# Softmax sums of a chunk inverted on 128 partitions after a DMA, values and sums copied off PSUM by ScalarE

## The chip, the cores and the metric

The kernel runs on one core of a Trainium2 chip. The metric is the device time of one execution in microseconds (us). Before the change it is 6243.12 us, the median of 3 runs (6239.61 to 6246.1). The engines are named as the profile names them: PE (TensorE matmuls) and PEld (its weight loads), DVE (VectorE), ACT (ScalarE), POOL (GpSimd) and SP, whose queue issues the DMAs.

## The reference

Two layers over `x` of 8 batches x 2048 rows x 256 features, each wrapped in a residual and a layer norm, with one 2048 x 2048 adjacency matrix `adj`. What matters here is the first layer, attention with 4 heads of 64 features whose softmax is taken apart in each **chunk** of 256 keys and then summed over the 8 chunks:

```python
kc = k.reshape(B, H, Nc, CHUNK, Dh)
vc = v.reshape(B, H, Nc, CHUNK, Dh)
scores = jnp.einsum('bhnd,bhjcd->bhnjc', q, kc) / sqrt(Dh)
scores = jnp.clip(scores, -10.0, 10.0)
scores = jnp.where(mask == 0, -10.0, scores)
attn = jax.nn.softmax(scores, axis=-1)          # over c, in one chunk j
ctx = jnp.einsum('bhnjc,bhjcd->bhnd', attn, vc) # sum over j and c
out = ctx @ Wo.T + bo + x                       # then layer norm, residual, layer norm
```

So each query row, head and chunk has a sum of exponentials of its own, and the values of a chunk have to be divided by it before chunks are added. The second layer is a graph attention with one softmax over all 2048 keys; the change doesn't touch its lines.

## The kernel before

It is written in a framework in which the program states the work in order and a scheduler in the build places each engine's instructions: an instruction can be put ahead of an earlier one that isn't ready, while each engine executes its list strictly in order. Buffers come from pools: tiles of one tag share `bufs` buffers, and a new tile waits until an old one is released.

**Setup** (about 170 us): weights are transposed, and two int8 masks for all of `adj` are kept in SBUF. Then a loop over the 8 batches runs, each about 757 us:

- four `x` tiles of 512 rows are loaded (L215, pool `xp`, 5 buffers), transposed on PE (L204, tiles `p_xT`), and projected to keys (`pk`, L225) and values (`pv`, L234).
- **attention**, in four blocks `ib` of 512 queries. A block projects its queries (`pq`, L250) and then goes through 16 key tiles `c` of 128, two to a chunk. `scores(c)` makes, for each pair of heads, a tile `sc` of 128 keys x 2 heads x 512 queries in PSUM (L262), which DVE clips and masks in place (L270) and ACT exponentiates into `e` (L272). `values(c)` multiplies `e` with the values into `u` and with ones into `d` (L288): 12 calls with 32 output columns each, so that `u` (128 x 1024) and `d` (128 x 512) hold the four heads on 32 partitions each, and the 32 rows of a head in `d` are all equal to its sum. Both accumulate over the two key tiles of a chunk. The loop states scores(c) ahead of values(c-1).
- When a chunk `j` is complete, DVE takes the reciprocal of all of `d` (L297) and multiplies `u` with it straight from PSUM (L300 for the first chunk, L303 after), and POOL adds the product `un` to `ctxT` (L304).
- After 16 key tiles the block projects `ctxT` (`po`, L319); the residual and both layer norms follow on DVE and POOL (L326 to L332) and overwrite the block's `x` tile.
- **graph attention** in four blocks (L356 to L420), which reads the `x` tile of a block for the last time at L418. It loads rows of a mask (`fb`, L361) into buffers of the tag `ctx`, the one of `ctxT`.

[...] the tag `two` has 3 buffers of two banks each, shared by the `sc` and `u` tiles; the tag `m` has 2 buffers of one bank, shared by `d`, `po`, `pq`, `p_xT`, `pk`, `pv` and other small results. In the trace, tiles of the tag `m` get their buffers in the order in which the program states them: `pq` of the next block runs after `po` of this one (1810.84 after 1805.63 us), although it needs nothing of it.

The SP queue carries loads of `x`, loads of `fb` and stores of the output, none inside a block of attention but the first `fb`.

Of the kernel before, what the change touches and what calls it, by code (L numbers as in the profile page):

```python
# [9 lines left out]
F32 = mybir.dt.float32  # L10
# [7 lines left out]
DRAM = bass.MemoryType.DRAM  # L18

P = 128  # L20
# [8 lines left out]
def tile_adj_attention__then__gat(  # L29
# [27 lines left out]
    nc = tc.nc  # L57
    B, N, F = x.shape
    H, D = 4, 64
# [3 lines left out]
    IB = 512  # L63
# [4 lines left out]
    DH = D // 2  # L68
    QSCALE = 1.0 / D**0.5

    const = ctx.enter_context(tc.tile_pool(name="const", bufs=1))
    dram = ctx.enter_context(tc.tile_pool(name="dram", bufs=1, space=DRAM))

    ps_2 = ctx.enter_context(tc.tile_pool(name="ps_2", bufs=3, space=PSUM))
    ps_m = ctx.enter_context(tc.tile_pool(name="ps_m", bufs=2, space=PSUM))
# [38 lines left out]
    with tc.tile_pool(name="setup", bufs=2) as setup:  # L114
        for name, w in (("q", Wq), ("k", Wk), ("v", Wv), ("o", Wo)):
            wn = setup.tile([P, KC, F], F32, tag="wn", name=f"wn_{name}")
            if name == "o":
                by_half = w.rearrange("(o p) (h k m) -> p o k h m", p=P, h=H, k=2)
                for o in range(KC):
                    for k in range(2):  # L120
                        nc.sync.dma_start(
                            out=wn[:, o, ts(k, P)].rearrange("p (h m) -> p h m", h=H), in_=by_half[:, o, k]
# [11 lines left out]
        for n in range(2):  # L134
            a_bc = setup.tile([P, F], F32, tag="a_bc", name=f"a_bc{n}")
            nc.sync.dma_start(
                out=a_bc, in_=a[n * F : (n + 1) * F, :].rearrange("f o -> (f o)").partition_broadcast(P)
# [31 lines left out]
                    nc.vector.tensor_scalar(to, pt, hi - lo, lo, ALU.mult, ALU.add)  # L169

    big = ctx.enter_context(tc.tile_pool(name="big", bufs=1))
    xp = ctx.enter_context(tc.tile_pool(name="xp", bufs=5))
    wp = ctx.enter_context(tc.tile_pool(name="wp", bufs=2))
    rp = ctx.enter_context(tc.tile_pool(name="rp", bufs=1))
    ep = ctx.enter_context(tc.tile_pool(name="ep", bufs=4))
    sp = ctx.enter_context(tc.tile_pool(name="sp", bufs=3))

# [12 lines left out]
    def normalize(dst, src, name):  # L190
        mv, rstd = stats(src, name)
        for t in range(TPB):
            nc.vector.tensor_scalar(  # L193
                dst[:, t, :], src[:, t, :], mv[:, t, 0:1], rstd[:, t : t + 1], ALU.subtract, ALU.mult
            )
# [12 lines left out]
    def bc_rows(v):  # L208
        return v.unsqueeze(1).to_broadcast([P, TPB, F])

    for b in range(B):
# [33 lines left out]
        for ib in range(NIB):  # L245
            qT = wp.tile([P, NPAIR, IB], F32, tag="q", name=f"qT{b}_{ib}")
            for o in range(NPAIR):
                pq = ps_m.tile([P, IB], F32, tag="m", name=f"pq{b}_{ib}_{o}")
                for k in range(KC):
                    nc.tensor.matmul(  # L250
                        pq, WT["q"][:, k, ts(o, P)], xT[:, k, ts(ib, IB)], start=(k == 0), stop=(k == KC - 1)
                    )
                nc.scalar.activation(qT[:, o, :], pq, AF.Identity, bias=bq_c[:, o : o + 1], scale=QSCALE)  # L253

            ctxT = wp.tile([P, 2, IB], F32, tag="ctx", name=f"ctxT{b}_{ib}")

            def scores(c):
                es = []
                for hp in range(NPAIR):
                    sc = ps_2.tile([P, 2, IB], F32, tag="two", name=f"sc{b}_{ib}_{hp}_{c}")  # L260
                    for h in range(2):
                        nc.tensor.matmul(  # L262
                            sc[:, h, :],
                            kT[h * D : (h + 1) * D, hp, ts(c, P)],
                            qT[h * D : (h + 1) * D, hp, :],
                            start=True,
                            stop=True,
                        )
                    cap = mask0[:, c, ts(ib, IB)].unsqueeze(1).to_broadcast([P, 2, IB])
                    nc.vector.scalar_tensor_tensor(sc, sc, -CLIP, cap, ALU.max, ALU.min)  # L270
                    e = ep.tile([P, 2, IB], F32, tag="e", name=f"e{b}_{ib}_{hp}_{c}")
                    nc.scalar.activation(e, sc, AF.Exp)  # L272
                    es.append(e)
                return es

            ud = {}

            def values(c, es):
                j, first, last = c // CPT, c % CPT == 0, c % CPT == CPT - 1
                if first:  # L280
                    ud["u"] = ps_2.tile([P, 2, IB], F32, tag="two", name=f"u{b}_{ib}_{j}")
                    ud["d"] = ps_m.tile([P, IB], F32, tag="m", name=f"d{b}_{ib}_{j}")
                u, d = ud["u"], ud["d"]
                for part in range(3):
                    for h in range(H):
                        rows = slice(h * DH, (h + 1) * DH)
                        f0 = h * D + part * DH
                        nc.tensor.matmul(  # L288
                            u[rows, part, :] if part < 2 else d[rows, :],
                            v[:, c, f0 : f0 + DH] if part < 2 else ones[:, 0:DH],  # L290
                            es[h // 2][:, h % 2, :],
                            start=first,
                            stop=last,
                        )
                if last:
                    r = rp.tile([P, IB], F32, tag="r", name=f"r{b}_{ib}_{j}")
                    nc.vector.reciprocal(r, d)  # L297
                    r2 = r.unsqueeze(1).to_broadcast([P, 2, IB])
                    if j == 0:
                        nc.vector.tensor_mul(ctxT, u, r2)  # L300
                    else:
                        un = wp.tile([P, 2, IB], F32, tag="un", name=f"un{b}_{ib}_{j}")
                        nc.vector.tensor_mul(un, u, r2)  # L303
                        nc.gpsimd.tensor_add(ctxT, ctxT, un)  # L304

            pending = []
            for c in range(NT):
                pending.append((c, scores(c)))
                if len(pending) > 1:
                    values(*pending.pop(0))  # L310
            for args in pending:
                values(*args)

            y = wp.tile([P, TPB, F], F32, tag="y", name=f"y{b}_{ib}")
            for t2 in range(TPB // 2):
                po = ps_m.tile([P, 2, F], F32, tag="m", name=f"po{b}_{ib}_{t2}")
                for j in range(2):
                    for k in range(KC):
                        nc.tensor.matmul(  # L319
                            po[:, j, :],  # L320
                            ctxT[:, k, ts(2 * t2 + j, P)],
                            WT["o"][:, k, :],
                            start=(k == 0),
                            stop=(k == KC - 1),
                        )
                nc.vector.tensor_add(y[:, ts(t2, 2), :], po, xs[ib][:, ts(t2, 2), :])  # L326
            nc.gpsimd.tensor_add(y, y, bc_rows(bo_bc))
            normalize(y, y, f"a{b}_{ib}")
            nc.gpsimd.tensor_mul(y, y, bc_rows(gamma_bc))
            nc.gpsimd.tensor_add(y, y, bc_rows(beta_bc))  # L330
            nc.gpsimd.tensor_add(y, y, xs[ib])
            normalize(xs[ib], y, f"b{b}_{ib}")  # L332
# [23 lines left out]
        for ib in range(NIB):  # L356

            mx = sp.tile([P, TPB], F32, tag="mx", name=f"mx{b}_{ib}")
            for t in range(TPB):
# [3 lines left out]
                    out=fb,  # L363
# [26 lines left out]
            for c in range(NT):  # L390

                e = ep.tile([P, 2, IB], F32, tag="e", name=f"g{b}_{ib}_{c}")
                w, z = e[:, 0, :], e[:, 1, :]
# [14 lines left out]
            r = sp.tile([P, TPB], F32, tag="rd", name=f"rd{b}_{ib}")  # L408
            ex = ep.tile([P, TPB, F], F32, tag="e", name=f"ex{b}_{ib}")
            for t in range(TPB):  # L410
                u = us[t // 2][:, t % 2, :]
# [35 lines left out]
```

## Time and profile before

| | |
|---|---|
| median of 3 runs | 6243.12 us |
| profiled execution | 6237.52 us |
| its span, first to last instruction | 6235.7 us |
| granted PE clock, mean | 0.884 |
| PE busy | 4793.9 us (77%) |
| DVE busy | 4091.7 us (66%) |
| ACT busy | 1939.1 us (31%) |
| POOL busy | 1020.9 us (16%) |
| DVE reciprocal of `d`, L297 | 256 x 3358 ns = 859.5 us |
| DVE product from PSUM, L300 and L303 | 256 x 1.21 us |
| DMA, share of 16 engines on the SP queue | 6.2% |

A busy share is an average over stages with different limits, so the reading is by stage. "Idle before" is the time that an engine stood still just before an instruction, with the one that ended the wait. In a row of the timeline the columns are start (us from the start of the span), duration (us), engine, line, operation, output<-input with sizes, the count of merged instructions and, in brackets, idle time and who ended it.

### The profile page before, as it was taken

The page shows a single profiled execution, that of the slowest core. Times are in us where ns is not written, and L with a number is a line of the kernel's source. Part 1 is how long each engine was busy: PE and PEld are TensorE (multiplying, and loading weights), DVE is VectorE, ACT ScalarE, POOL GpSimd, SP SyncE. Part 2 cuts the span into 40 slices and gives each one's busy share as a digit, 9 for nine tenths or more (in the row PEclk, how much of TensorE's full clock was granted, in tenths as well). Part 3 has the DMA queues.
Part 4 walks back from the last instruction along what each step waited for, and adds up shares of the span by engine and source line. Part 5 has one row for each costly group of instructions (what it writes and reads, how often), then busy time and mean ns, then how long its engine had stood idle before and what let it go on. Part 6 is the DMA issues. An engine that isn't in the chain of part 4 may idle for free. (4 is left out here: it accounts for less than half of the span.)

```text
span 6235.7 us, 59188 instructions
## 1 busy us (share of the span) xinstructions
PE 4793.9 (77%) x24080; PEld 2176.6 (35%) x24080; DVE 4091.7 (66%) x5126; ACT 1939.1 (31%) x2433; POOL 1020.9 (16%) x486
## 2 busy tenths in 40 slices
PE   5877787777877778777787768877788776887767
PEld 4222362224622255222552226422263222632236
DVE  8566676666766676665766658665586565856658
ACT  0222252222422234222342224322253222522224
POOL 0112111221022210222102120122101221012111
PEclk9888898888988889888898889988899888998889
DMA  5000110001000010000100001000020000100010
GB/s 192 1 1 4 38 41 1 1 4 54 24 1 1 4 58 21 1 1 4 61 17 1 1 7 61 14 1 4 4 66 10 1 4 21 51 4 1 4 34 31
DMA packets 61713, 131.73 MB, mean 21 GB/s; under 512 B 6400, under 2 KB 40960, under 8 KB 59392
## 3 DMA queue, kind: packets, MB, share of 16 engines
q1 hardware_dynamic: 61440, 127.94, 6.2%
q8 instruction: 189, 3.10, 0.2%
q14 instruction: 84, 0.69, 0.0%
HBM read 102.76 MB, written 25.17 MB: 21 GB/s over the span
## 5 line engine op out<-in xcount | busy, mean ns | idle before, releaser
L272 ACT ACTIVATE e<-sc 128x1024 f32<-128x1024 f32 x1024 | 1048.8, 1024 | 2384.7 <-DVE sc L270 2201.7
L288 PE MATMUL u<-e,v 128*32 128x512 f32 x8192 | 1299.9, 770 | 615.2 <-ACT e L272 615.2
L270 DVE SCALAR_TENSOR_TENSOR sc<-sc,mask 128x1024 f32<-128x1024 f32 x1024 | 1225.7, 1220 | 653.6 <-PE sc L262 653.2
L262 PE MATMUL sc<-qT,kT 64*128 64x512 f32 x4096 | 1076.9, 646 | 162.4 <-ACT e L272 162.4
L297 DVE RECIPROCAL r<-d 128x512 f32<-128x512 f32 x256 | 859.5, 3358 | 403.0 <-PE d L288 403.0
L399 PE MATMUL us<-wh,g 128*128 128x257 f32 x4096 | 964.7, 395 | 145.8 <-ACT g L397 145.3
L304 POOL TENSOR_TENSOR ctxT<-ctxT,un 128x1024 f32<-128x1024 f32 x224 | 527.6, 2356 | 3208.1 <-DVE un L303 3208.1
L399 PEld LDWEIGHTS us<-wh,g 128*128 128x128 f32 x4096 | 788.9, 196 | 322.1 <-ACT g L397 210.1
L288 PEld LDWEIGHTS u<-e,v 128*32 128x32 f32 x8192 | 257.7, 131 | 1537.5 <-ACT e L272 859.8
L262 PEld LDWEIGHTS sc<-qT,kT 64*128 64x128 f32 x4096 | 366.6, 195 | 943.6 <-issue 483.8
L288 PE MATMUL d<-e,ones 128*32 128x512 f32 x4096 | 538.8, 598 | 0.0
L395 DVE SCALAR_TENSOR_TENSOR g<-ab,sij,g 128x512 f32<-128x512 f32 x512 | 422.6, 843 | 39.3 <-ACT g L394 38.7
L394 ACT ACTIVATE g<-ab,sj 128x512 f32<-128x512 f32 x512 | 364.0, 718 | 187.6 <-PE us L399 176.3
L397 ACT ACTIVATE g<-g 128x512 f32<-128x512 f32 x512 | 315.5, 622 | 236.1 <-DVE g L396 234.0
L319 PE MATMUL po<-WT_o,ctxT 128*128 128x256 f32 x512 | 171.5, 507 | 234.3 <-POOL ctxT L304 234.3
L396 DVE TENSOR_TENSOR g<-g,mask 128x512 f32<-128x512 f32 x512 | 342.3, 683 | 5.2
L362 DVE CUSTOM_DVE_ANT_0 fb<-sj_row,fb 128x2048 bf16<-128x2048 f32 x128 | 291.3, 2285 | 75.0 <-ACT sj_row L354 55.6
L418 POOL TENSOR_TENSOR hx<-hx,x 128x1024 f32<-128x1024 f32 x32 | 84.0, 2624 | 1463.2 <-DVE hx L417 972.1
L303 DVE TENSOR_TENSOR un<-u,r 128x1024 f32<-128x1024 f32 x224 | 271.4, 1212 | 3.7 <-DVE r L297 0.5
L288 PEld LDWEIGHTS d<-e,ones 128*32 128x32 f32 x4096 | 111.1, 111 | 357.3 <-issue 357.3
L319 PEld LDWEIGHTS po<-WT_o,ctxT 128*128 128x128 f32 x512 | 132.7, 267 | 289.3 <-POOL ctxT L304 263.3
L253 ACT ACTIVATE qT<-pq,bq_c 128x512 f32<-128x512 f32 x64 | 44.0, 687 | 588.0 <-PE pq L250 588.0
(92 smaller groups left out, 2912.4 us busy)
## 6 DMA issues: line engine op xcount, KB each, us to landing
fb<-far SPq DMA_DIRECT2D x128, 512.0 KB, 3.3
araw<-in_adj_dram SPq DMA_DIRECT2D x16, 1024.0 KB, 4.9
x<-in_x_dram SPq DMA_DIRECT2D x32, 512.0 KB, 3.9
out_dram<-hx SPq DMA_DIRECT2D x32, 512.0 KB, 2.9
far<-fb SPq DMA_DIRECT2D x16, 512.0 KB, 3.2
wn_q<-in_L_gnn_Wq_dram SPq DMA_DIRECT2D x1, 256.0 KB, 5.0
wn_k<-in_L_gnn_Wk_dram SPq DMA_DIRECT2D x1, 256.0 KB, 5.2
W_aug<-in_L_gnn_W_dram SPq DMA_DIRECT2D x1, 256.0 KB, 5.4
```

What stands on the lines that cost most here:

```text
L262: nc.tensor.matmul(sc[:, h, :], kT[h * D : (h + 1) * D, hp, ts(c, P)], qT[h * D : (h + 1) * D, hp, :], start=True, stop=True,)
L270: nc.vector.scalar_tensor_tensor(sc, sc, -CLIP, cap, ALU.max, ALU.min)
L272: nc.scalar.activation(e, sc, AF.Exp)
L288: nc.tensor.matmul(u[rows, part, :] if part < 2 else d[rows, :], v[:, c, f0 : f0 + DH] if part < 2 else ones[:, 0:DH], es[h // 2][:, h % 2 ...
L297: nc.vector.reciprocal(r, d)
L304: nc.gpsimd.tensor_add(ctxT, ctxT, un)
L319: nc.tensor.matmul(po[:, j, :], ctxT[:, k, ts(2 * t2 + j, P)], WT["o"][:, k, :], start=(k == 0), stop=(k == KC - 1),)
L394: nc.scalar.activation(z, ab[:, 1, :], AF.Identity, bias=sj2[:, c : c + 1])
L395: nc.vector.scalar_tensor_tensor(z, ab[:, 0, :], sij[:, c, 1:2], z, ALU.add, ALU.max)
L396: nc.vector.tensor_tensor(z, z, mask1[:, c, ts(ib, IB)], ALU.min)
L397: nc.scalar.activation(w, z, AF.Exp)
L399: nc.tensor.matmul(us[t // 2][:, t % 2, 0 : F + 1], w[:, ts(t, P)], wh[:, c, :], start=(c == 0), stop=(c == NT - 1),)
```

## The change

Three pools change, and the end of a chunk is written anew:

- `xp` goes from 5 to 4 buffers, `rp` from 1 to 2 (and holds a second tag), and a pool of 3 small DRAM tiles is added.
- When a chunk is complete, ACT copies `u` to `un` and `d` to `ds`, both in SBUF. A DMA takes one of the 32 equal rows of each head and spreads its 512 sums over 32 partitions, 16 to each: `dc`, 128 x 16. DVE takes the reciprocal of `dc`. A second DMA writes it to a DRAM tile `rd` of 4 rows x 512, and a third reads each row back onto the 32 partitions of its head: `r`, 128 x 512. All three are issued on SP.
- The product and the sum into `ctxT` come in `normalized()`, which the program states one chunk later, behind the copies of the next chunk; the last two chunks of a block get theirs after its loop. The product now reads `un` and `r`, both in SBUF, and writes `un` in place.

```diff
+    rows_d = ctx.enter_context(tc.tile_pool(name="rows", bufs=3, space=DRAM))
...
-    xp = ctx.enter_context(tc.tile_pool(name="xp", bufs=5))
+    xp = ctx.enter_context(tc.tile_pool(name="xp", bufs=4))
...
-    rp = ctx.enter_context(tc.tile_pool(name="rp", bufs=1))
+    rp = ctx.enter_context(tc.tile_pool(name="rp", bufs=2))
...
-                if last:
-                    r = rp.tile([P, IB], F32, tag="r", name=f"r{b}_{ib}_{j}")
-                    nc.vector.reciprocal(r, d)
-                    r2 = r.unsqueeze(1).to_broadcast([P, 2, IB])
-                    if j == 0:
-                        nc.vector.tensor_mul(ctxT, u, r2)
-                    else:
-                        un = wp.tile([P, 2, IB], F32, tag="un", name=f"un{b}_{ib}_{j}")
-                        nc.vector.tensor_mul(un, u, r2)
-                        nc.gpsimd.tensor_add(ctxT, ctxT, un)
+                if not last:
+                    return
+                un = wp.tile([P, 2, IB], F32, tag="un", name=f"un{b}_{ib}_{j}")
+                nc.scalar.copy(un, u)
+                ds = rp.tile([P, IB], F32, tag="ds", name=f"ds{b}_{ib}_{j}")
+                nc.scalar.copy(ds, d)
+                dc = sp.tile([P, IB // DH], F32, tag="dc", name=f"dc{b}_{ib}_{j}")
+                nc.sync.dma_start(
+                    out=dc,
+                    in_=ds.rearrange("(h m) (n w) -> h m n w", m=DH, n=DH)[:, 0, :, :],
+                )
+                nc.vector.reciprocal(dc, dc)
+                rd = rows_d.tile([H, IB], F32, tag="rd", name=f"rdr{b}_{ib}_{j}")
+                nc.sync.dma_start(out=rd.rearrange("h (m w) -> (h m) w", m=DH), in_=dc)
+                r = rp.tile([P, IB], F32, tag="r", name=f"r{b}_{ib}_{j}")
+                nc.sync.dma_start(
+                    out=r,
+                    in_=rd.unsqueeze(1).to_broadcast([H, DH, IB]),
+                )
+                chunks.append((j, un, r))
+
+            chunks = []
+
+            def normalized():
+                j, un, r = chunks.pop(0)
+                r2 = r.unsqueeze(1).to_broadcast([P, 2, IB])
+                if j == 0:
+                    nc.vector.tensor_mul(ctxT, un, r2)
+                else:
+                    nc.vector.tensor_mul(un, un, r2)
+                    nc.gpsimd.tensor_add(ctxT, ctxT, un)
 
             pending = []
             for c in range(NT):
                 pending.append((c, scores(c)))
                 if len(pending) > 1:
                     values(*pending.pop(0))
+                if len(chunks) > 1:
+                    normalized()
             for args in pending:
                 values(*args)
+            while chunks:
+                normalized()
```

## The prediction

> **What bounds the kernel now.** I read the waits first, then the timeline of one attention chunk, then the two seams around it: the end of a block, and the start of a batch. A row of the waits gives who waited for whom: us in total, times, longest.
>
> ```profile
> ACT e L272 <- DVE sc L270: 2201.7, 716, 6.1
> ...
> PE u L288 <- ACT e L272: 615.2, 224, 2.8
> ```
>
> ACT waits for DVE and PE waits for ACT, 224 times for about 2.75 us each: once in nearly every chunk. One chunk, PE and then DVE:
>
> ```profile
> 1740.93 1.99 PE L262 MATMUL sc<-qT,kT 64*128 64x512 f32 x8
> 1742.85 1.92 PE L288 MATMUL u<-e,v 128*32 128x512 f32 x16
> 1744.59 1.04 PE L288 MATMUL d<-e,ones 128*32 128x512 f32 x8
> 1745.57 1.99 PE L262 MATMUL sc<-qT,kT 64*128 64x512 f32 x8
> 1747.48 1.06 PE L288 MATMUL d<-e,ones 128*32 128x512 f32 x8
> 1751.29 3.43 PE L288 MATMUL u<-e,v 128*32 128x512 f32 x16 [2.75 <-ACT e L272]
> ```
>
> ```profile
> 1745.70 3.36 DVE L297 RECIPROCAL r<-d 128x512 f32<-128x512 f32 x1 [1.23 <-PE d L288]
> 1748.98 1.21 DVE L270 SCALAR_TENSOR_TENSOR sc<-sc,mask 128x1024 f32<-128x1024 f32 x1
> 1750.09 1.21 DVE L303 TENSOR_TENSOR un<-u,r 128x1024 f32<-128x1024 f32 x1
> 1751.22 1.22 DVE L270 SCALAR_TENSOR_TENSOR sc<-sc,mask 128x1024 f32<-128x1024 f32 x1
> ```
>
> The chunk is complete at 1745.6. DVE then inverts for 3.36 us while the next scores, ready at about 1746.7, wait for their clip until 1748.98. The new `u` finds no PSUM buffer: the old one is held until the product ends (1751.30), another until the first exp ends (1751.24). PE idles and then runs `u` in 3.43 us instead of 1.92. The reciprocals of this block are 13.6 to 13.9 us apart; while PE doesn't wait, one key tile takes 1745.57 - 1740.93 = 4.64 us, a chunk 9.28. The reciprocal is on the path here; DVE at 66% overall doesn't say so. The end of a block, PE and then DVE:
>
> ```profile
> 1797.29 1.03 PE L288 MATMUL d<-e,ones 128*32 128x512 f32 x8
> 1805.63 5.37 PE L319 MATMUL po<-WT_o,ctxT 128*128 128x256 f32 x16 [7.30 <-POOL ctxT L304]
> ```
>
> ```profile
> 1798.40 3.36 DVE L297 RECIPROCAL r<-d 128x512 f32<-128x512 f32 x1 [4.88 <-PE d L288]
> 1801.86 1.23 DVE L303 TENSOR_TENSOR un<-u,r 128x1024 f32<-128x1024 f32 x1
> ```
>
> PE stands for 7.3 us while reciprocal, product and POOL's sum follow one another, and the next block's `pq` is queued behind `po`. The start of a batch:
>
> ```profile
> 1661.14 1.04 PE L204 MATMUL p_xT<-ident,x 128*128 128x128 f32 x8
> ...
> 1668.59 0.37 SPq L215 DMA_DIRECT2D x<-in_x_dram  x1
> ```
>
> The last `x` tile is transposed at 1661.14, having been loaded at 1631.2. The load at 1668.59 takes the buffer that the last L418 has just released, and is already for the batch after.
>
> [...] the 512 KB store lands 2.9 us after issue, of which its packets fill some 1.3, so 1.6 here. [...]
>
> **The change, part by part.** Let T be the end of a chunk's last `d`.
>
> *Reciprocal.* Gone: 256 x 3.358 = 859.5 us of DVE. In its place 128x16: 16/512 of 3.36 plus the 0.16 of the smallest reciprocal (L412), about 0.25.
>
> *ACT copies.* `u`: 1.02 (as the exp of that size); `d`: 0.59 (L205). 256 x 1.61 = 412 us on ACT, inside the 2384.7 us that it idles before exps. Queued behind them are the next exps, ready at about T+2.5; the copies end by T+1.3. Without that cover they cost up to 1.6 a chunk. They release `u` by about T+0.7, before PE asks at T+1.9: the 2.75 us wait and the cold 1.5 us go.
>
> *DMA chain.* `dc`: 128 packets of 64 B; 4 B packets took 9 ns, 128 B 13, so it is fixed cost: between 1.6 and the 3.2 of `bv_bc`, taken as 2.0. `rd`: 1.6 to 3.2 (`far<-fb`), taken as 1.9. `r`: 256 KB in 2 KB packets; [...] (1 KB packets took 46 ns, 4 KB 159); taken as 3.8. L, from T until `r` is there: 1.3 copies + 0.3 reciprocal + 0.2 hops + 7.7 = 9.5; from 7.9 to 13.0.
>
> *SP.* 768 issues at about 0.37 us each, 284 us in an empty stretch. SP waits for ACT, DVE and the second landing in turn; behind these waits stand the next chunk's DMAs and the first `fb` loads, needed much later. `x` loads and stores come after the blocks. Nothing.
>
> *New DVE waits.* The reciprocal waits for `dc` (about T+3.4): the clips of the next scores come at T+1.2 to T+3.6, those after at T+5.8, so it falls in a gap. The product of chunk j waits for `r` and, as stated, stands after the clips that end at about T+8.2 and before one due at T+P+1.2, with P the period. It ends at L+1.25. PE bears a clip about 1.0 late (first exp ends 3.6 after the scores start, next scores start at 4.64). So P is the larger of 9.28 and L-0.95. With L 9.5 the chain is hidden; P = 9.28, and I take 9.6 for hops. What is late next is PE itself.
>
> *Block.* Before, the first reciprocal to the last: 1836.17 to 1928.12, 91.95 us. After: 6 x 9.6 and a last one of 1.91 + 2.72 + 2.72 = 7.4, together 65.0. Gain 26.95.
>
> *End of a block.* The chain lies bare. `ds` ends at T+0.7 as ACT is free, so `r` at L-0.6; product 1.25, sum 2.36, hops 0.25: `po` at L+3.3 = 12.8 instead of 7.3. Loss 5.5. [...] 32 x (26.95 - 5.5) = 686 us.
>
> *xp 5 to 4.* The last `x` tile of the next batch now waits for the last L418: issue 1668.59 + 3.9 to land = 1672.5 instead of 1661.1, 11.4, and a cold start, 1.5. `pk` gets its PSUM buffer behind these transposes, as `pq` does behind `po`. 7 x 12.9 = 90 us. If `pk` passes them it is nothing.
>
> *Other pools.* `un` is held until POOL's sum, T+13, and needed again at T+2P: nothing. `rp` and the DRAM tiles: nothing. Graph attention is untouched.
>
> Sum: 6237.5 (the profiled execution, span 6235.7) - 686 + 90 = 5641; the median of the runs shown lies 5.6 higher, so about 5645.
>
> **The rivals.** *Partly hidden, 0.20.* [...] hops are longer, L = 12: P = 11.05, a block gains 18.25 and loses 8.0: 32 x 10.25 - 90 = 238, so 6000. Much the same results if the new `u` still gets the first exp's buffer: P = 11, about 5910. [...] against: 80 ns packets are cheap, and `u` is released first.
>
> *Slower, 0.16.* The latency of three dependent DMAs stands in DVE's list ahead of the clips. Each us of L costs 32 x 7 = 224 us once P follows it; from L = 13.1, over 3.8 per DMA, it is slower than before. At the 4.7 that the 1 KB `bk_c` took, L = 15.9, P = 14.95: a block loses 5.2 and 11.9, 32 x 17.1 + 90 = 637, 6880. A reciprocal placed ahead of the clips would decide it sooner. For it: setup DMAs of 1 to 256 KB took 4.7 to 5.4; against: they queued behind one another, and lone ones of 512 KB took 2.9 to 3.9.
>
> *Nothing, 0.04.* L near 13, gains and losses cancel, about 6235.
>
> **How the numbers follow.** The forecast has 0.60: from 5530 (L 8, P 9.28) to 5775 (P 10.2, `po` 6 later); without the loss at `xp` down to 5440. Range 5480 to 6200: it takes in the partly hidden case and leaves out the slower one and the lowest corner. A measurement tells about 0.2% (12 us) from no change; faster 0.80, same 0.03, slower 0.17, with the last case split.
>
> **What would show it.** Right: the wait of `u` for `e` gone, `u` near 1.92 us everywhere, chunks 9.3 to 10 us apart, PE's wait at `po` near 13 us and at `p_xT` near 12 per batch, ACT up by 412 us, DVE down by about 800. Wrong: DVE's products or reciprocals waiting for DMAs with clips behind them, chunks over 11 us apart, or `pk` ahead of the last transposes. I would be most wrong if a 64 B spread takes 4 us.

## The result and the profile after

The changed kernel takes 6268.71 us (median of 5 runs, 6265.88 to 6272.06), the kernel before 6242.61 us (5 runs, 6239.61 to 6246.1): ratio 1.0042, 95% interval 1.0027 to 1.0057. It is slower by 0.4%, where 9.6% less time was predicted. Most of what the change was priced at did happen: DVE is busy for 3323.2 us in place of 4091.7, ACT for 2281.0 in place of 1939.1. The time didn't follow, so the waits come first.

```profile
ACT e L273 <- DVE sc L271: 1519.0, 523, 5.9
...
DVE un L327 <- DMA r<-rdr: 888.2, 224, 8.3
...
PE po L347 <- POOL ctxT L328: 471.6, 32, 16.8
...
PE u L289 <- ACT e L273: 457.4, 191, 5.3
```

The wait of `u` for `e`, which was to go, is still there: 457.4 us in place of 615.2. What was new and not expected at such a size is DVE's own wait: 224 products wait for the DMA of `r`, 4.0 us each. One chunk in the timeline, first DVE, then ACT, SP and PE, over the same stretch (L271 is the clip, L273 the exp, L327 the product, L301 and L303 the copies of `u` and `d`, L305, L311 and L313 the three DMAs):

```profile
1743.14 1.23 DVE L327 TENSOR_TENSOR un<-un,r 128x1024 f32<-128x1024 f32 x1 [3.49 <-DMA r<-rdr]
1744.28 3.49 DVE L271 SCALAR_TENSOR_TENSOR sc<-sc,mask 128x1024 f32<-128x1024 f32 x3
1748.89 0.25 DVE L309 RECIPROCAL dc<-dc 128x16 f32<-128x16 f32 x1 [1.13 <-DMA dc<-ds]
1752.22 1.23 DVE L271 SCALAR_TENSOR_TENSOR sc<-sc,mask 128x1024 f32<-128x1024 f32 x1 [3.08 <-PE sc L263]
1755.98 1.22 DVE L327 TENSOR_TENSOR un<-un,r 128x1024 f32<-128x1024 f32 x1 [2.52 <-DMA r<-rdr]
1757.12 3.48 DVE L271 SCALAR_TENSOR_TENSOR sc<-sc,mask 128x1024 f32<-128x1024 f32 x3
```

```profile
1741.08 1.01 ACT L301 COPY un<-u 128x1024 f32<-128x1024 f32 x1 [0.37 <-PE u L289]
1745.54 1.02 ACT L273 ACTIVATE e<-sc 128x1024 f32<-128x1024 f32 x1 [3.45 <-DVE sc L271]
1746.46 0.58 ACT L303 COPY ds<-d 128x512 f32<-128x512 f32 x1
```

```profile
1747.07 0.54 SPq L305 DMA_DIRECT2D dc<-ds  x1
1749.18 0.32 SPq L311 DMA_DIRECT2D rdr<-dc  x1
1750.61 0.54 SPq L313 DMA_DIRECT2D r<-rdr  x1
```

```profile
1740.83 1.04 PE L289 MATMUL d<-e,ones 128*32 128x512 f32 x8
1741.80 1.99 PE L263 MATMUL sc<-qT,kT 64*128 64x512 f32 x8
1746.62 2.59 PE L289 MATMUL u<-e,v 128*32 128x512 f32 x16 [2.83 <-ACT e L273]
```

Call the chunk whose `d` ends here (T = 1740.83 + 1.04 = 1741.87) j. Follow the ring. On DVE the product of chunk j-1 waits for its `r` until 1743.14, and a clip of the scores that PE needs next stands behind it. That clip feeds the exp at 1745.54. On ACT, behind that exp, stands the copy of j's **sums**: it runs at 1746.46, though `d` was complete 4.6 us earlier. Only then do the three DMAs of chunk j start, `r` is there at 1755.98, and the product of j stands again between the clips of a tile. So one turn of the ring is 0.6 copy + 1.8 `dc` + 0.3 reciprocal + 1.4 `rd` + 5.4 `r` + 1.1 product + 1.3 clip + 0.9 exp = 12.8 us, which is how far apart the products are (1755.98 - 1743.14 = 12.84). PE, which needs 9.28 us for a chunk, waits. Over all blocks the products are 12.6 us apart (the last one of a block left out), so this turn is a usual one.

The end of a block, DVE, the last `dc` on SP and then PE, and the start of a batch on PE:

```profile
1805.47 1.23 DVE L327 TENSOR_TENSOR un<-un,r 128x1024 f32<-128x1024 f32 x1 [6.27 <-DMA r<-rdr]
1806.62 0.25 DVE L309 RECIPROCAL dc<-dc 128x16 f32<-128x16 f32 x1
1813.06 1.23 DVE L327 TENSOR_TENSOR un<-un,r 128x1024 f32<-128x1024 f32 x1 [6.19 <-DMA r<-rdr]
```

```profile
1802.83 0.54 SPq L305 DMA_DIRECT2D dc<-ds  x1
```

```profile
1801.00 1.04 PE L289 MATMUL d<-e,ones 128*32 128x512 f32 x8
1816.82 6.68 PE L347 MATMUL po<-WT_o,ctxT 128*128 128x256 f32 x16 [14.78 <-POOL ctxT L328]
```

```profile
1663.56 1.04 PE L205 MATMUL p_xT<-ident,x 128*128 128x128 f32 x8
1674.96 1.94 PE L205 MATMUL p_xT<-ident,x 128*128 128x128 f32 x8 [10.37 <-DMA x<-in_x_dram]
```

PE stands 14.8 us at the end of a block in place of 7.3, and the transposes of a batch stand 10.4 us for the last `x` tile. At the end of a block the chain lies bare, and one thing more holds it: the last `dc`, issued at 1802.83, takes 1.8 us, but its reciprocal stands on DVE behind the product of the chunk before, which waits for its own `r`, and runs at 1806.62, 2.0 us late (1.6 on average). Means over all blocks and batches, from PE's records (the third column is the kernel of experiment 12, below):

| us | before | after | product one clip later |
|---|---|---|---|
| chunk to chunk, from end of `d` to end of `d`, without the last of a block | 13.46 | 12.02 | 9.47 |
| start of `pq` to the block's last `d` | 115.35 | 105.67 | 88.31 |
| last `d` to `po` | 7.32 | 14.74 | 13.09 |
| duration of `po` | 5.36 | 5.91 | 5.91 |
| last `po` of a batch to next `pk` | 220.0 | 231.9 | 231.9 |

Before to after: a block gains 9.7 and loses 7.4 + 0.55, 32 x 1.7 = 55 us gained; seven batch starts lose 11.9 each, 83, and from `pk` to `pq` each of the eight batches takes 1.1 us more, some 9 (28.7 in place of 27.65). Sum +37; the spans differ by 34.5.

### The profile page after: what moved, and what is told of

It reads as the page before. It is cut to its first block, busy times and chain, and to the rows that moved or that the text cites. A ratio compares the mean times of both kernels' runs of the same rounds, so it can differ in the third digit from the quotient of the medians.

```text
span 6270.2 us, 61066 instructions
## 1 busy us (share of the span) xinstructions
PE 4662.4 (74%) x24080; PEld 2201.4 (35%) x24080; DVE 3323.2 (53%) x5126; ACT 2281.0 (36%) x2945; POOL 1017.3 (16%) x486
## 5 line engine op out<-in xcount | busy, mean ns | idle before, releaser
L273 ACT ACTIVATE e<-sc 128x1024 f32<-128x1024 f32 x1024 | 1031.9, 1031 | 1693.9 <-DVE sc L271 1519.0
L271 DVE SCALAR_TENSOR_TENSOR sc<-sc,mask 128x1024 f32<-128x1024 f32 x1024 | 1212.9, 1224 | 544.4 <-PE sc L263 518.4
L289 PE MATMUL u<-e,v 128*32 128x512 f32 x8192 | 1145.1, 683 | 457.6 <-ACT e L273 457.4
L327 DVE TENSOR_TENSOR un<-un,r 128x1024 f32<-128x1024 f32 x224 | 274.4, 1225 | 888.2 <-DMA r<-rdr 888.2
L289 PEld LDWEIGHTS u<-e,v 128*32 128x32 f32 x8192 | 236.6, 118 | 1257.6 <-ACT e L273 655.8
L289 PE MATMUL d<-e,ones 128*32 128x512 f32 x4096 | 572.0, 632 | 0.0
L347 PE MATMUL po<-WT_o,ctxT 128*128 128x256 f32 x512 | 189.0, 548 | 471.6 <-POOL ctxT L328 471.6
L301 ACT COPY un<-u 128x1024 f32<-128x1024 f32 x256 | 258.9, 1011 | 185.1 <-PE u L289 185.0
L289 PEld LDWEIGHTS d<-e,ones 128*32 128x32 f32 x4096 | 145.0, 121 | 373.5 <-issue 373.5
```

The lines of the kernel that those rows point to most:

```text
L289: nc.tensor.matmul(u[rows, part, :] if part < 2 else d[rows, :], v[:, c, f0 : f0 + DH] if part < 2 else ones[:, 0:DH], es[h // 2][:, h % 2 ...
L347: nc.tensor.matmul(po[:, j, :], ctxT[:, k, ts(2 * t2 + j, P)], WT["o"][:, k, :], start=(k == 0), stop=(k == KC - 1),)
```

## The experiments

The theory after the traces: the chain of DMAs is short enough to be hidden; what isn't hidden comes of two lists of instructions, DVE's and ACT's, that close a ring round it (the expectations call it the loop). Rivals: the DMAs' own latency sets the period wherever things stand; or one of the parts that came along (`xp`, ScalarE's copies) eats the gain.

**1 and 2: the `x` buffers alone, and all but them.** e1 is the kernel before with four, e2 the changed one with five.

```diff
-    xp = ctx.enter_context(tc.tile_pool(name="xp", bufs=5))
+    xp = ctx.enter_context(tc.tile_pool(name="xp", bufs=4))
```

> The kernel before with xp cut from 5 to 4 buffers and nothing else. Loop theory (the new chunk end gains a little, the cut of xp gives it back): the last x tile of each next batch waits for the last L418, 7 batch starts lose about 13 us each, so about 6242 + 92 = 6334 us. Rival (the time was lost in the chunk end alone, projections pass the late transposes): 6242 us, no change.

> The changed kernel with xp back at 5 buffers. Loop theory: 6269 - 92 = about 6177 us, 1% below the kernel before, with 10 us of wait at the last transposes of a batch gone. Rival (chunk end alone): 6269 us, no change.

e1: 6326.57 us, ratio to before 1.0144 (1.0127 to 1.0161). e2: 6197.89, ratio 0.9932 (0.9917 to 0.9947). The buffer costs 70 to 85 us; the rest of the change gains 0.7% in place of the 11% that the prediction gave it (686 us). The buffer's price, 90 us, was about right, so the failure is in the chunks and the ends of the blocks.

**3: only the order on DVE.** The product of chunk j is issued behind both clips of tile 2j+5, the second tile of chunk j+2.

```diff
-                if len(chunks) > 1:
-                    normalized()
+                if len(chunks) > 1 and c % 2 == 1:
+                    with tc.issue_after(clips[0].ins):
+                        normalized()
```

(`clips[0]` is the last clip of the tile; in 8, 10, 11 and 12 too.)

> The changed kernel with DVE's order alone altered: the product of a chunk is issued behind both clips of the key tile after the next (the second clip of tile 2j+5), instead of between the two clips of tile 2j+4. Same operations, same DMAs. Loop theory (product waits for r, a clip waits behind it, an exp for the clip, the copy of the sums stands behind that exp on ACT and starts the next chain): the loop is cut, chunks 12.5 to about 9.5 us apart, 32 x 6 x 3 = 576 us less, about 5690 us; the wait at po stays near 14.7. Rival (ACT's two copies, the PSUM handover or PE's clock set the chunk): chunks stay over 12 us apart, 6200 to 6270 us.

5667.68 us, ratio 0.9083 (0.9069 to 0.9096); chunks 9.44 us apart (12.02), `po` after 13.75. Same instructions, same DMAs, same four `x` buffers: the order alone is worth 601 us (on ACT's list, see 12). The DMAs' latency by itself is not the bound.

**4: no wait for `r`.** All of the chain runs, but the product takes a constant, so the division by the sums is left out.

```diff
-                j, un, r = chunks.pop(0)
-                r2 = r.unsqueeze(1).to_broadcast([P, 2, IB])
+                j, un, _ = chunks.pop(0)
+                r2 = r0.unsqueeze(1).to_broadcast([P, 2, IB])
```

> The changed kernel in which the product multiplies by a constant tile instead of r: the division by the sums is left out, all copies, DMAs and reciprocals are still issued. Loop theory: nobody waits for r, chunks about 9.5 us apart, and the wait at po falls from 14.7 to about 5: 576 + 32 x 9.7 = 886 us less, about 5380 us. Rival (copies, PSUM, clock): only the wait at po falls, about 5960 us.

A single run: 5360.81 us, chunks 9.45 us apart, `po` after 4.05. The copies, the DMAs' issues and traffic cost nothing that a chunk shows; the wait for `r` is all of it, in the chunks and at the end of a block.

**5: the product on POOL**, in the changed kernel, so that nothing on DVE waits for `r`.

```diff
-                    nc.vector.tensor_mul(ctxT, un, r2)
+                    nc.gpsimd.tensor_mul(ctxT, un, r2)
...
-                    nc.vector.tensor_mul(un, un, r2)
+                    nc.gpsimd.tensor_mul(un, un, r2)
```

> The changed kernel with the product un x r moved from DVE to POOL, so that no clip stands behind a wait for r; ACT's copies and the three DMAs stay. Loop theory: chunks 9.4 to 9.6 us apart, the wait at po up by about 1 us to 15.5: about 6269 - 32 x 6 x 2.5 + 32 = 5820, to 5700 with a shorter last chunk. Rival (ACT's copies, PSUM, clock): chunks stay at 12, about 6300 us.

5698.61 us, ratio 0.9133 (0.912 to 0.9147), chunks 9.47 us apart. POOL now waits for `r`, with nothing behind it that PE needs before the end of a block (`po` after 14.45). It is another way to take the product out of the clips' list, with the same effect.

**6: the matmuls of `d` ahead of those of `u`**, to have the sums copied sooner.

```diff
-                for part in range(3):
+                for part in (2, 0, 1):
```

> The changed kernel with the ones-matmuls of d stated ahead of those of u, so that the sums are complete 1.8 us earlier and their copy is issued ahead of the exp that waits for the late clip; the build then puts the product ahead of both clips of tile 2j+4, still ahead of clips. Loop theory: the part of the loop in which the sums' copy stands behind the exp goes (4.6 us), what is left is a product that waits for r ahead of two clips: chunks about 9.9 us apart, wait at po near 13: 5830 us. If the product's place on DVE alone is the cause, ACT's order doesn't matter: chunks stay at 12 and the time near 6210.

6229.1 us, ratio 0.9981 (0.9972 to 0.999): a miss. The build placed the product ahead of both clips of a tile, and the copy of the sums stands behind an exp all the same (that exp waited 5.64 us for its clip). Chunks 12.11 us apart: the ring wasn't opened. The time is near the second theory's 6210, but the run doesn't decide, as the copy wasn't freed.

**7 and 8: no DMAs in a chunk.** Only ScalarE's copy of `u` is kept; DVE inverts all of `d` from PSUM, 3.36 us, as before. In 7 the product comes a chunk later, as in the changed kernel. In 8 reciprocal and product are issued behind both clips of tile 2j+3, whose scores PE computes just after chunk j is complete, and `xp` has 5 buffers.

```diff
-                ds = rp.tile([P, IB], F32, tag="ds", name=f"ds{b}_{ib}_{j}")
-                nc.scalar.copy(ds, d)
...
                 r = rp.tile([P, IB], F32, tag="r", name=f"r{b}_{ib}_{j}")
-                nc.sync.dma_start(
-                    out=r,
-                    in_=rd.unsqueeze(1).to_broadcast([H, DH, IB]),
-                )
+                nc.vector.reciprocal(r, d)
```

> The changed kernel without the DMA chain: ACT still copies u to SBUF, DVE takes the reciprocal of d straight from PSUM over 128x512 as before the change, the product reads the copy; xp stays at 4. Loop theory: no round trip anywhere, u is released early, the 3.36 us reciprocal holds one clip by about 2.2 us of which PE bears 1: chunks about 10.4 us apart, wait at po back to about 7.3: 6327 (kernel before with xp 4) - 32 x 6 x 3.0 = 5750 us. Rival (the costly reciprocal is what the path needs shortened): chunks stay near 13.5, 6327 us.

> ACT copies u, no DMA chain, reciprocal and product on DVE issued behind both clips of the key tile after the chunk, xp at 5. Loop theory: DVE needs 4 x 1.22 + 3.36 + 1.23 = 9.5 us in a chunk, PE 9.3, so chunks 9.5 to 10.3 us apart and the wait at po 7.3: 6242 - 32 x (6 x 3.4 + 2) = 5530 us, to 5450. Rival (the copy itself is what costs): no better than the copy-only run less 71 us for xp.

7: 5747.19 us, ratio 0.9209 (0.9195 to 0.9223), chunks 10.63 us apart. 8: 5352.92 us, ratio 0.8577 (0.8564 to 0.859), chunks 9.36 us apart and `po` 7.85 after the last `d`. DVE of 8:

```profile
1699.05 2.36 DVE L271 SCALAR_TENSOR_TENSOR sc<-sc,mask 128x1024 f32<-128x1024 f32 x2 [0.25 <-PE sc L263]
1701.32 3.35 DVE L310 RECIPROCAL r<-d 128x512 f32<-128x512 f32 x1
1704.59 1.21 DVE L271 SCALAR_TENSOR_TENSOR sc<-sc,mask 128x1024 f32<-128x1024 f32 x1
1705.70 1.21 DVE L315 TENSOR_TENSOR un<-un,r 128x1024 f32<-128x1024 f32 x1
```

DVE is nearly full (0.25 us idle at 1699.05) and PE, at 9.36 us a chunk, is the bound. The long reciprocal that the change does away with never had to go: with `u` copied off PSUM early (7) and the reciprocal behind the clips that are due (8), the same 3.35 us cost PE almost nothing. This version beats both kernels; the order without the copy wasn't run.

**9: the second exp behind the copy of the sums**, an attempt to cut the ring on ACT (one edge added from the exp of the second half of tile 2j+2 to the copy).

```diff
+                if c < NT - 1:
+                    tc.add_manual_dep(exps[0].ins, dcopy.ins.name, ...)
```

> The changed kernel with one edge more: on ACT the exp of the second half of the next key tile is issued behind the copy of the sums, so the copy no longer stands behind an exp that waits for a clip behind a product. The build answers by placing the product of chunk j ahead of both clips of the first tile of chunk j+2 (in the changed kernel it stands between them). Theory (a loop through two lists: product ahead of a clip on DVE, the sums' copy behind that clip's exp on ACT; cutting either link opens it): the copy of the sums ends about 0.7 us after the chunk's last d instead of about 5, r is there at about 10, and the product still stands ahead of clips, so chunks 10 to 10.5 us apart instead of 12.0, and about 5950 to 6000 us. Rival (only the product's place on DVE matters, and it now stands one clip earlier): no gain or a loss, 6270 or more. Rival (the chain of DMAs by itself, 9 to 10 us, sets the period wherever the copy stands): as the theory at best, but then the wait for r stays above 3 us per chunk.

6476.04 us, ratio 1.0383 (1.0367 to 1.0398): a miss, and slower. ACT and DVE:

```profile
1773.31 1.01 ACT L302 COPY un<-u 128x1024 f32<-128x1024 f32 x1 [0.43 <-PE u L290]
1774.22 0.59 ACT L304 COPY ds<-d 128x512 f32<-128x512 f32 x1
...
1786.06 1.02 ACT L273 ACTIVATE e<-sc 128x1024 f32<-128x1024 f32 x1 [6.93 <-DVE sc L271]
1786.98 1.01 ACT L302 COPY un<-u 128x1024 f32<-128x1024 f32 x1
1787.88 0.60 ACT L304 COPY ds<-d 128x512 f32<-128x512 f32 x1
```

```profile
1783.66 1.23 DVE L333 TENSOR_TENSOR ctxT<-un,r 128x1024 f32<-128x1024 f32 x1 [5.58 <-DMA r<-rdr]
1784.81 2.36 DVE L271 SCALAR_TENSOR_TENSOR sc<-sc,mask 128x1024 f32<-128x1024 f32 x2
```

The build moved the product ahead of both clips, so now the **first** exp waits for it (6.93 us), and both copies stand behind that one. The ring is the same with the copy of `u` added: 1787.88 - 1774.22 = 13.66 us. Chunks are 13.11 us apart on average. My edge moved the link and didn't cut it. The time fits the first rival (6270 or more), but this run doesn't decide for it.

**10: `r` by four DMAs**, one for each head, on the kernel of 3, to see whether its 256 KB come sooner in four parts.

```diff
-                nc.sync.dma_start(
-                    out=r,
-                    in_=rd.unsqueeze(1).to_broadcast([H, DH, IB]),
-                )
+                for h in range(H):
+                    nc.sync.dma_start(
+                        out=r[h * DH : (h + 1) * DH, :],
+                        in_=rd[h, :].partition_broadcast(DH),
+                    )
```

> The kernel with the product placed behind the clips, but r read by four DMAs, one for each head[...]. It separates why the DMA of r took 5.3 us where 3.8 was forecast. [...] r is complete some 1 us sooner in spite of three issues more (about 0.5 each), and the wait at po falls from 13.75 to between 11.5 and 13 us, for about 5610 to 5650 us beside 5668. If the 5.3 us are latency[...]: the wait at po grows by the three issues to about 15, about 5680 to 5710 us.

5628.43 us, ratio 0.9024 (0.901 to 0.9037), `po` after 12.09 (13.75). The last `r` of a block, SP and DVE:

```profile
1731.63 1.69 SPq L315 DMA_DIRECT2D r<-rdr  x4
```

```profile
1735.00 1.23 DVE L329 TENSOR_TENSOR un<-un,r 128x1024 f32<-128x1024 f32 x1 [4.87 <-DMA r<-rdr]
```

From the first issue to the product 3.37 us; where products wait for `r` it is 3.4 at the median, in place of 5.1 in experiment 3. The same 256 KB come sooner in spite of three issues more, so the 5.1 us aren't latency alone. In the packets of the two traces `r` is 128 packets of 2 KB, 84 ns each at the median, and on average 3.7 of them are under way at once in experiment 3, 6.6 here. What sets these two numbers no run shows.

**11: the last chunk of a block without DMAs** (reciprocal of 128x512 from PSUM), on the kernel of 3, with five `x` buffers.

```diff
+                if j == NT // CPT - 1:
+                    nc.vector.reciprocal(r, d)
+                    nc.vector.tensor_mul(un, u, r.unsqueeze(1).to_broadcast([P, 2, IB]))
+                    nc.gpsimd.tensor_add(ctxT, ctxT, un)
+                    return
```

> The kernel with the product placed behind the clips, with five x buffers again, and with the last chunk of each block normalized as in the kernel before (reciprocal of 128x512 straight from PSUM, no DMAs), since nothing covers the DMAs there. Theory: what the change still loses after its loop is opened is the bare chain at the end of a block (13.75 us from the last d to po, 7.3 before) and the x buffer (about 80 us). With the wait back at 7.3 to 8.5: 5668 - 80 - 32 x 5.5 = about 5410, between 5390 and 5450 us, about the time of the version without any DMA (5353) or a little above it. Rival (po waits for the product of the chunk before the last, whose chain is bare too): the wait at po stays above 10 us, and about 5500 us.

5546.25 us, ratio 0.8886 (0.8871 to 0.8901), `po` after 12.28: the rival is nearer. The product of the chunk before the last waits for its own bare chain, and the last reciprocal stands behind it on DVE. Five `x` buffers give most of the gain.

**12: one clip later.** The place where the prediction had put the product: behind the second clip of tile 2j+4, not between its two clips.

```diff
                 if len(chunks) > 1:
-                    normalized()
+                    with tc.issue_after(clips[0].ins):
+                        normalized()
```

> The changed kernel with the product of chunk j placed one clip later on DVE: behind the second clip of tile 2j+4 in place of between its two clips, which is where the prediction had put it (after the clips that end at about T+8.2, before the one due at T+P+1.2). ACT then has both exps of tile 2j+2, the copy of the values, the copy of the sums. Theory (the place of the product by one clip is the step of the prediction that failed; with the product where it was assumed, its rule P = the larger of 9.28 and L - 0.95 holds): the sums are copied at about T+0.8, r is there at L = 10.2, so P = 9.3 to 9.6 and about 5670 to 5720 us. Rival (any product that waits for r ahead of clips still to come holds the loop, and only the placement behind tile 2j+5 freed it): chunks 10.3 to 11 us apart, between 5870 and 6050 us.

5665.94 us, ratio 0.9081 (0.9067 to 0.9094), chunks 9.47 us apart. The end of a chunk on PE, then DVE and ACT:

```profile
1701.65 1.04 PE L290 MATMUL d<-e,ones 128*32 128x512 f32 x8
```

```profile
1703.05 1.23 DVE L328 TENSOR_TENSOR un<-un,r 128x1024 f32<-128x1024 f32 x1 [1.48 <-DMA r<-rdr]
1704.19 1.23 DVE L271 SCALAR_TENSOR_TENSOR sc<-sc,mask 128x1024 f32<-128x1024 f32 x1
1705.87 0.25 DVE L310 RECIPROCAL dc<-dc 128x16 f32<-128x16 f32 x1 [0.45 <-DMA dc<-ds]
1706.04 1.21 DVE L271 SCALAR_TENSOR_TENSOR sc<-sc,mask 128x1024 f32<-128x1024 f32 x1
1708.50 2.36 DVE L271 SCALAR_TENSOR_TENSOR sc<-sc,mask 128x1024 f32<-128x1024 f32 x2 [1.25 <-PE sc L263]
1712.40 1.23 DVE L328 TENSOR_TENSOR un<-un,r 128x1024 f32<-128x1024 f32 x1 [1.54 <-DMA r<-rdr]
```

```profile
1700.47 2.16 ACT L273 ACTIVATE e<-sc 128x1024 f32<-128x1024 f32 x2 [1.67 <-DVE sc L271]
1702.52 1.01 ACT L302 COPY un<-u 128x1024 f32<-128x1024 f32 x1
1703.41 0.60 ACT L304 COPY ds<-d 128x512 f32<-128x512 f32 x1
```

The chunk's last `d` ends at T = 1702.69. The copies end at T+1.3, the pair of clips at 1708.50 ends at T+8.2, `r` is there at T+9.7 and the product follows. It still waits for `r` in nearly every chunk, 614.5 us in all, and PE isn't held up by it: a wait is free as long as what is queued behind it isn't due. One clip is worth 603 us. ACT's list changed with it, here and in 3 and 5: the copy of `u` now stands behind the second exp too. That is no gain of its own, since the copy of the sums stands behind this exp in the changed kernel as well; it comes sooner because the exp isn't late.

**13: both exps behind the copies.** This does free the copy on ACT, and leaves the product ahead of the clips.

```diff
+                if c < NT - 1:
+                    for exp in exps:
+                        tc.add_manual_dep(exp.ins, dcopy.ins.name, ...)
```

> The changed kernel with both exps of tile 2j+2 issued on ACT behind the copy of the sums of chunk j, so that no exp that waits for a product stands ahead of it (in the run that put only the second exp behind it, the first one took over that part). The build places the product of chunk j ahead of both clips of tile 2j+4. This leaves the product ahead of the clips on DVE and cuts the loop on ACT alone. Theory A (cutting the ACT link alone is enough to open the loop, the product's place matters little then): r at about 9.6 us after the last d, the exps held to 0.7 us after it cost PE about 1 us a chunk, so chunks 10.2 to 10.8 us apart, 5850 to 6000 us. Theory B (the scores of tile 2j+4 are ready 2.7 us before the end of chunk j+1, and a product ahead of their clips must end about 1 us before that chunk's end: P = L + 1.25 + 0.7 with L = 9.6): chunks 11.3 to 12.4 apart, 6100 to 6350 us, so that moving the product is the cure and moving the copies is not.

6120.88 us, ratio 0.9815 (0.9799 to 0.9832), chunks 11.58 us apart: the numbers of theory B. DVE, a `dc` on SP, and PE:

```profile
1754.75 1.23 DVE L336 TENSOR_TENSOR un<-un,r 128x1024 f32<-128x1024 f32 x1 [6.75 <-DMA r<-rdr]
1755.89 3.49 DVE L271 SCALAR_TENSOR_TENSOR sc<-sc,mask 128x1024 f32<-128x1024 f32 x3
1759.29 0.24 DVE L318 RECIPROCAL dc<-dc 128x16 f32<-128x16 f32 x1
```

```profile
1754.78 0.54 SPq L314 DMA_DIRECT2D dc<-ds  x1
```

```profile
1754.32 1.13 PE L263 MATMUL sc<-qT,kT 64*128 64x512 f32 x4 [0.33 <-ACT un L302]
1758.23 1.94 PE L263 MATMUL sc<-qT,kT 64*128 64x512 f32 x4 [2.78 <-ACT e L273]
```

With the copy free, PE still waits for an exp whose clip stands behind the product. The next reciprocal stands behind product and clips too (1759.29, with its `dc` issued at 1754.78), so `r` is there 10.9 us after the last `d` on average and not theory B's 9.6: its period came out, its way of getting there only in part. Freeing ACT gains 148 us, moving the product by one clip 603. The place of the product is the cause; the copy behind the exp makes it worse.

## Why the prediction was wrong

*New DVE waits: the step that failed.* The product was put "after the clips that end at about T+8.2 and before one due at T+P+1.2". The build put it **between** those two clips, both of tile 2j+4. The second of them is then due near T+7, ahead of any `r` at T+9.5, and the rule P = max(9.28, L - 0.95) doesn't hold: chunks were 12.02 us apart in place of 9.6, with clips behind the waiting product, the first sign of being wrong that the prediction named. In experiment 12 the product has the stated place, and the terms come out: P 9.47 (9.6 taken), L 9.7 (9.5 taken), a block shorter by 115.35 - 88.31 = 27.0 us (26.95, in part by luck: the last chunk took 8.35 where 7.4 was taken), and 5666 us in all (5645). No run has this place and an L long enough to test the rule's other branch. With the 14.1 of the turn shown the branch gives 13.15, not far from 12.8, but that is no support: this L has the ring's own wait in it. The program states the product behind both clips; the list that the build makes has it one place earlier, and the prediction took the order from the program without pricing the neighbouring places.

*ACT copies.* "The copies end by T+1.3", with the exps behind them: wrong here, and a result of the first. The copy of the sums stood behind an exp and ended at T+5.2. That is 3.9 of the 4.6 us by which L (14.1) passes 9.5. In experiment 12 it stands behind the same exp and ends at T+1.3. Their durations, 1.01 and 0.58 us, were right.

*DMA chain.* 7.7 us taken; 8.6 in the turn shown, 8.1 in experiment 12. `dc` 1.8 (2.0) and `rd` 1.4 (1.9) were less, `r` 5.4 and 4.8 more (3.8; 5.0 on average in both kernels). The 3.8 was the author's estimate, as was the range of L, 7.9 to 13.0. The packets of a 512 KB store fill about 1.65 us of its 2.9 in the kernel before, which leaves 1.25 where the prediction had 1.6 as its low end.

*End of a block.* 5.5 us of loss taken, 7.4 measured (5.8 with the product one clip later). `r` cost 1.2 more, and the last reciprocal stood 1.6 behind the product of the chunk before, a wait that the prediction's sum left out; `dc` and `rd` gave 0.7 back. *xp.* 90 us taken; 83 and 9 in the accounts, 85 in experiment 1, 71 in experiment 2: about right. The "cold" 1.5 is the 3.43 us of `u` after its wait less the 1.92 without one; the transposes behind the 10.4 us wait took 1.94 us where another eight took 1.04 without one. `pk` does wait behind the last transposes. *SP, other pools.* Nothing taken, nothing seen (experiment 4).

*The rivals.* The slower one named the mechanism, latency of the DMAs in DVE's list ahead of the clips, but asked for more than 3.8 us per DMA. They took 2.9 on average in the turn shown; the order did it. Its 0.16 was too little for a kernel with a scheduler whose list hadn't been seen.

The mean of 12.02 and the ring's 12.8 go together: between the first two chunks of a block no product waits yet, and they are 9.39 us apart; the five distances after that are 12.55 on average. What stays open: why single distances vary so (9.4 to 15.2 us, tenth and ninetieth percentile) while the products come evenly (12.2 to 13.2), and why the build places a product that waits for a DMA between two clips.

## What to carry to other kernels

When a step is split by a DMA, ask for its second half which instructions stand behind it on its in-order engine, and when they are due; here one place in the list was worth 603 us. Then follow the list of each engine that starts the transfer: if its trigger stands behind something that the second half delays, latency is not hidden but goes round in a ring, and freeing one link may move it (experiment 9) or gain little (13). Before making a long instruction shorter, try it unchanged behind what is due: here that, with `u` copied off PSUM by ACT, gained 14%.

## What the runs showed of the hardware

- In the changed kernel a DMA of 256 KB from 4 rows of DRAM to 128 partitions took 5.0 us from issue to use on average (4.7 to 5.4 in most), with 3.7 of its 2 KB packets under way at once; as four DMAs of 64 KB (experiment 10) 3.4 us at the median, with 6.6.
- DMAs of 8 KB between SBUF and SBUF, or to DRAM, took 1.8 and 1.4 us from issue to use (median), less than the 2.0 and 1.9 taken.
- The product with two SBUF inputs took 1.22 us (1.21 from PSUM), and POOL's sums 2.34 us. None of the 256 products ran while POOL summed, so these are the times of each alone.
